# Whitening products of the last stage: six of eight as 64x64 parts, in place of four of eight

## The chip, the cores and the metric

The kernel runs on one core of a Trainium2 chip. The core has a matrix engine (TensorE, PE in the profile), a vector engine (VectorE, DVE), a scalar engine (ScalarE, ACT), GpSimd (POOL) and a queue engine (SyncE, SP) that here only issues DMA transfers. TensorE writes its products into PSUM, a memory of eight banks of 512 float32 for each of 128 partitions; VectorE or ScalarE move them from there into SBUF, which is called an eviction here; DMA carries SBUF to and from HBM.

The metric is the time of one execution on the device in microseconds (us), as the median of several. A profile is one further execution, taken by the hardware profiler, and has its own time.

## The reference

Everything is float32. The input x has 4 images of 256 channels and 64 x 64 pixels. Two layers follow one another. The first is a local attention: a dilated 7 x 7 convolution (256 to 128 channels) and a 1 x 1 convolution (128 to 49) give 49 logits for each pixel, a softmax over the 49 gives weights, and the output is the weighted sum of 49 shifted copies of x. The second layer whitens the result over groups of 64 channels:

```python
x = jnp.transpose(X, (1, 0, 2, 3)).reshape(g, nc, -1)      # g = 4 groups of nc = 64 channels
xc = x - x.mean(-1, keepdims=True)
Sigma = EPS * I + jnp.einsum('gdm,gem->gde', xc, xc) / m
rTr = (1.0 / jnp.einsum('gii->g', Sigma))[:, None, None]
Sigma_N = Sigma * rTr
P = I
for _ in range(T_ITERS):                                    # 5
    P3 = jnp.einsum('gij,gjk,gkl->gil', P, P, P)
    P = 1.5 * P - 0.5 * jnp.einsum('gij,gjk->gik', P3, Sigma_N)
xn = jnp.einsum('gde,gem->gdm', P * jnp.sqrt(rTr), xc)      # the last stage of the kernel
```

then multiplies by a weight and adds a bias for each channel. The covariance is a sum over all pixels of all images, so the last einsum can begin only when the whole attention layer is done.

## The kernel before

**Layout.** Channels lie on the 128 partitions, in two blocks of 128 (`cc`), and each block holds two whitening groups of 64. The attention output stays in SBUF in eight tiles, `slots[2*b + pr]`, for image `b` and row parity `pr`: 128 partitions x 2 blocks x 32 rows x 64 columns. Three of them were moved to HBM while the attention ran and come back as `back` tiles.

**Stages.** The convolutions and the attention take most of the time. Then `whiten` (generators for both blocks in turn) makes the matrices: `wm[cc]`, 128 x 128 and block diagonal with a 64 x 64 block for each group, a scale `sc[cc]` and an offset `beta[cc]` for each channel, and `abx[cc]`, which is scale and offset with the two groups' partitions exchanged. The last stage multiplies every pixel by `wm` and stores the result.

**The last stage (L1410 to L1457).** Its loops run over 4 images, 2 channel blocks and `q` in (0, 2): 16 groups. A group covers 16 rows of each parity, as four products of 128 channels x 512 pixels: `y[pr][k]`, with parity `pr` and half `k`. It gathers them in two SBUF tiles `st[0]` and `st[1]`, 128 x 8 x 2 x 64, of which each is stored by one transfer of 512 KB (`store(k)`, on SP's queue). The `out` pool has six such tiles.

A product is made in one of two ways:
- *plain* (`plain(k)`, L1429): one 128 x 128 matmul into a one-bank tile `tp` (three of them), and one eviction of 128 x 512 with `sc` and `beta`.
- *as parts* (L1445): since `wm` is block diagonal, only its two 64 x 64 blocks matter. Two products are made at once, by four 64 x 64 matmuls, one in each quarter of the array. For `k = 0` group G0 goes to PSUM partitions 0 to 63 and G1 to 64 to 127 (*straight*). For `k = 1` the groups cross: G0's result lands on G1's partitions and the other way round. The straight bank is evicted in one instruction of 128 x 512. The crossed bank needs two instructions of 64 x 512, one for each half, since each writes to other partitions than it reads, with `abx`.

In every group before the change, the two products of parity 0 are plain and the two of parity 1 are parts.

**PSUM.** Parts use two banks, a *set* here. There are two sets: a two-bank tile `apply`, taken anew from a pool with one buffer, and the two long-lived one-bank tiles `cv`. `two_banks` gives them out in turn, so before the change the sets alternate from group to group.

**What sets the order.** `pe(...)` keeps TensorE's instructions in program order. `out_rows` (L1393 to L1398) gives evictions to ScalarE and VectorE in turn, counting all of them: odd to ScalarE, even to VectorE. In which order each of the two engines then takes its evictions is decided by the framework's planner when the kernel is built, from its own costs; each engine runs its queue strictly in that order. The framework also adds all the waits between engines, among them those that keep two engines from reading one PSUM bank at a time, and the wait of a matmul for the evictions that empty its bank.

The matmuls are float32, and each is carried out as two weight loads and two passes of 512 columns: the profile counts a plain product as two MATMUL rows and the four parts as eight.

Of the kernel before, what the change touches and what calls it, by code (L numbers as in the profile page):

```python
# [32 lines left out]
def kernel(  # L33
# [29 lines left out]
    nc = tc.nc  # L63
# [28 lines left out]
    def pe(ins):  # L92
        return tc.keep_in_program_order(ins)
# [9 lines left out]
    def tp():  # L103
        return ps_tp.tile([P, 512], F32, tag="tp", name="tp")
# [19 lines left out]
    store = []  # L124
# [27 lines left out]
    t = tp()  # L152
# [3 lines left out]
    t = tp()  # L156
# [5 lines left out]
    for k in range(2):  # L162
        t = ps_cv.tile([P, 512], F32, name=f"cv{k}")
# [53 lines left out]
    for k, c0 in enumerate(range(0, P, CB)):  # L217
        n = min(CB, P - c0)
        t = cv_buf[k % 2]
        for cc in range(NCC):  # L220
# [5 lines left out]
                    start=True, stop=True,  # L226
# [8 lines left out]
    for k0 in range(0, KT, TB):  # L235
        n = min(TB, KT - k0)
        t = tp()
# [1056 lines left out]
    wm, sc, beta, abx = {}, {}, {}, {}  # L1294
# [98 lines left out]
    def out_rows(o, i, scale, bias):  # L1393
        n[0] += 1
        if n[0] % 2:
            nc.scalar.activation(o, i, AF.Identity, bias=bias, scale=scale)
        else:
            nc.vector.tensor_scalar(o, i, scale, bias, ALU.mult, ALU.add)  # L1398

    def two_banks():  # L1400
        while True:
            t = ps_y.tile([P, 2, NT], F32, tag="y", name="apply")
            yield [t[:, k] for k in range(2)]
            yield cv_buf

    G0, G1 = slice(0, GW), slice(GW, P)
    two = two_banks()
    for b in (3, 2, 1, 0):
        for cc in range(NCC):
            for q in range(0, SH // TR, 2):  # L1410
                st = [
                    rpool.tile([P, TR, 2, W], F32, tag="out", name=f"out_{b}_{cc}_{q + k}", bufs=6)
                    for k in range(2)
                ]
                y = [
                    [
                        slots[2 * b + pr][:, cc, (q + k) * TR : (q + k + 1) * TR, :].rearrange(
                            "p r w -> p (r w)"
                        )
                        for k in range(2)  # L1420
                    ]
                    for pr in range(2)
                ]
                rows_of = lambda t: t.rearrange("p (r w) -> p r w", w=W)
                ts = next(two)

                def plain(k):
                    t = tp()
                    pe(nc.tensor.matmul(t, wm[cc], y[0][k], start=True, stop=True))  # L1429
                    out_rows(st[k][:, :, 0, :], rows_of(t), sc[cc], beta[cc])  # L1430

                def store(k):
                    nc.sync.dma_start(
                        out[
                            b, cc * P : (cc + 1) * P, 2 * (q + k) * TR : 2 * (q + k + 1) * TR, :
                        ],
                        st[k].rearrange("p r two w -> p (r two) w"),
                    )

                plain(0)  # L1440
                for k in range(2):
                    for i in (G0, G1):
                        o = i if k == 0 else (G1 if i is G0 else G0)
                        pe(
                            nc.tensor.matmul(  # L1445
                                ts[k][o], wm[cc][i, i], y[1][k][i],
                                start=True, stop=True, skip_group_check=True,
                            )
                        )
                out_rows(st[0][:, :, 1, :], rows_of(ts[0]), sc[cc], beta[cc])  # L1450
                store(0)
                for i, o in ((G1, G0), (G0, G1)):
                    out_rows(
                        st[1][o][:, :, 1, :], rows_of(ts[1])[i], abx[cc][i, 0:1], abx[cc][i, 1:2]
                    )
                plain(1)
                store(1)  # L1457


# [29 lines left out]
```

## Time and profile before

| what | value |
|---|---|
| median of 3 runs | 747.56 us (745.64 to 749.41) |
| the profiled execution | 746.19 us, of which the span from first to last instruction is 744.4 us |
| busy over the span | PE 94%, PEld 71%, DVE 82%, ACT 45%, POOL 7% |
| first matmul of the last stage | 689.5 us from the span's start |
| first and last store issued | 693.9 and 739.7 us |
| last eviction ends | 739.6 us |
| granted TensorE clock | 0.5 from 690.1 to 693.5 us, then full to 741.3 us |
| stores of the stage | 32 of 512 KB, 16.8 MB |

Times inside the profile are counted from the span's start. PE rows are matmul passes, PEld rows weight loads. A row of the timeline gives start, duration, engine, source line, operation, output<-input, shapes and count, and in brackets how long the engine stood idle before and what ended that. Consecutive alike instructions are merged into one row (x4, x8). The end of a matmul is modelled, so that the distance between the starts of matmuls is the better measure of their cost.

### The profile page before, as it was taken

Reading aid. Unit: us, or ns where it says so; the run is one execution under the profiler, and the core shown is the slowest. Engines: PE = TensorE matmul, PEld = TensorE weight load, DVE = VectorE, ACT = ScalarE, POOL = GpSimd, SP = SyncE. Lnnn points to the kernel's source line nnn. Section 1 sums busy time; section 2 is a strip of 40 time slices with the busy share of each in tenths; the row PEclk is TensorE's granted clock in tenths of the full one; section 3 lists DMA queues with packets and bytes.
Section 4 is the critical chain, followed back from the end, with each engine's and each line's share of the span. In section 5 each row is a group of like instructions: output and inputs, shape, how many; then the busy total and the mean of one; then the engine's idle time right before and its main releaser. Section 6 shows DMA issues by size and latency. Waiting matters only on the chain.

```text
span 744.4 us, 18491 instructions
## 1 busy us (share of the span) xinstructions
PE 703.4 (94%) x7512; PEld 528.3 (71%) x7512; DVE 611.3 (82%) x1268; ACT 332.5 (45%) x953; POOL 51.6 (7%) x52
## 2 busy tenths in 40 slices
PE   6999999997999897999999999999999889998996
PEld 1449543377898794799998958898998678885331
DVE  3789998999999989968995999799969655535575
ACT  1424240255364543466444435735535663322564
POOL 0410070020001110001000100000000000000000
PEclk9999999999899999999999999999999999999999
DMA  8991120147263491076545820534423144371588
GB/s 319 250 319 73 60 88 12 60 147 212 87 193 112 146 317 48 21 245 199 185 128 201 253 69 7 166 108 135 155 64 95 32 149 118 104 296 72 219 357 327
DMA packets 59629, 114.41 MB, mean 154 GB/s; under 512 B 22887, under 2 KB 42008, under 8 KB 58776
## 3 DMA queue, kind: packets, MB, share of 16 engines
q1 hardware_dynamic: 55848, 94.36, 38.7%
q0 software_dynamic: 3696, 18.88, 7.3%
q8 instruction: 59, 0.97, 0.5%
q14 instruction: 26, 0.21, 0.1%
HBM read 65.88 MB, written 47.33 MB: 152 GB/s over the span
## 4 chain that ended last, share of the span: by engine, by line
PE 61%; DVE 28%; ACT 4%; issue 3%; DMA 2%; SPq 0%; DVEq 0%; ACTq 0%
PE cv L538 20%; PE y L1061 12%; PE acc L685 6%; PE tp L1429 4%; PE tp L1093 3%; PE sig L1114 3%; PE cv L685 3%; PE tp L1032 3%; DVE xh L313 3%; DVE pv L313 3%; DVE zz L313 2%; DVE rb L313 2%; PE cv L222 2%; DVE ct L313 2%; DVE band L1009 2%
## 5 line engine op out<-in xcount | busy, mean ns | idle before, releaser
L538 PE MATMUL cv<-xh,wr 128*49 128x128 f32 x4368 | 250.2, 276 | 5.7 <-DVE rm L899 5.3
L538 PEld LDWEIGHTS cv<-xh,wr 128*49 128x49 f32 x4368 | 244.1, 124 | 9.6 <-ACT xh L494 5.5
L1061 PE MATMUL y<-band,xb 128*128 128x224 f32 (+2 forms) x640 | 150.6, 373 | 7.6 <-ACT xb L1040 5.9
L1061 PEld LDWEIGHTS y<-band,xb 128*128 128x128 f32 x640 | 109.1, 192 | 29.0 <-ACT xb L1040 8.9
L548 ACT COPY pv<-cv 113x486 f32<-113x486 f32 (+1 forms) x63 | 30.0, 476 | 86.1 <-PE cv L538 85.8
L1080 ACT ACTIVATE slot<-y,pivot 128x512 f32<-128x512 f32 x53 | 36.6, 738 | 63.5 <-PE y L1061 63.4
L1101 ACT COPY yt<-tp 128x256 f32<-128x256 f32 x128 | 45.6, 378 | 38.8 <-PE tp L1093 37.6
L1032 PE MATMUL tp<-ident,slot 128*128 128x128 f32 x256 | 49.9, 297 | 6.7 <-ACT yt L1101 6.7
L313 DVE SCALAR_TENSOR_TENSOR pv<-pv 113x162 f32<-113x162 f32 x186 | 54.9, 318 | 1.0 <-ACT pv L548 0.4
L1093 PE MATMUL tp<-ident,slot 128*128 128x128 f32 x256 | 52.1, 299 | 3.6 <-ACT yt L1101 1.0
L1009 DVE STREAM_TRANSPOSE band<-band 128x864 f32<-128x864 f32 (+1 forms) x48 | 47.4, 990 | 9.5 <-DMA band<-sd 9.5
L1093 PEld LDWEIGHTS tp<-ident,slot 128*128 128x128 f32 x256 | 41.3, 205 | 13.8 <-issue 4.4
L1032 PEld LDWEIGHTS tp<-ident,slot 128*128 128x128 f32 x256 | 39.9, 205 | 13.0 <-ACT yt L1101 8.0
L941 ACT COPY zt<-d 32x112 f32<-32x112 f32 (+2 forms) x156 | 44.8, 287 | 1.9
L893 ACT ACTIVATE d<-tp,mx 128x49 f32<-128x49 f32 x128 | 37.0, 336 | 17.4 <-DVE mx L888 13.9
L313 DVE SCALAR_TENSOR_TENSOR xh<-ct 128x512 f32<-128x512 f32 x42 | 27.8, 683 | 14.1 <-PE cv L538 13.7
L1114 PE MATMUL sig<-yt 128*64 128x65 f32 x1024 | 36.9, 225 | 0.0
L1114 PEld LDWEIGHTS sig<-yt 128*64 128x64 f32 x1024 | 32.4, 137 | 6.0 <-issue 4.5
L1040 ACT COPY xb<-tp 128x256 f32<-128x256 f32 x87 | 30.5, 376 | 12.9 <-PE tp L1032 12.4
L1040 DVE COPY xb<-tp 128x256 f32<-128x256 f32 x41 | 16.5, 421 | 23.5 <-PE tp L1032 23.5
L685 PE MATMUL acc<-slot,tap 128*49 128x496 f32 (+3 forms) x168 | 34.6, 569 | 0.0
L893 ACT ACTIVATION_READ_ACCUMULATOR d<-tp,mx 128x1 f32 x128 | 30.6, 241 | 0.0
(222 smaller groups left out, 959.2 us busy)
## 6 DMA issues: line engine op xcount, KB each, us to landing
out_dram<-out SPq DMA_DIRECT2D x32, 512.0 KB, 3.4
sd<-zt SPq DMA_DIRECT2D x16, 896.0 KB, 4.2
slot<-in_x_dram POOLq DMA_DIRECT2D x12, 1024.0 KB, 10.0
band<-sd SPq DMA_DIRECT2D x128, 84.0 KB, 2.2
wr<-gd SPq DMA_DIRECT2D x15, 588.0 KB, 3.7
wr<-gd SPq DMA_DIRECT2D x15, 490.0 KB, 3.9
spill<-slot POOLq DMA_DIRECT2D x3, 2048.0 KB, 7.7
back<-spill SPq DMA_DIRECT2D x3, 2048.0 KB, 13.3
```

The costliest lines, as they stand in the source:

```text
L313: return in_turn(STT(o, a, f, b, ALU.mult, ALU.add))
L538: nc.tensor.matmul(cv[h * HB : h * HB + KT, k, sr : sr + n, sc : sc + n], wv[:, sc, sr, cc], xh[bc][:, :n, h * NCC + cc, :n], start=(j == ...
L685: nc.tensor.matmul(ps[h * HB : h * HB + KT, :, w0:w1_], w[v][:, cc], xs[:, :, cc, w0 + d : w1_ + d], start=(j == 0), stop=(j == len(order) ...
L893: nc.scalar.activation(d[:, h, i], lt[i // NI][:, i % NI, h, :KT], AF.Exp, bias=mx[:, i, h : h + 1], accum_out=s[:, h, i : i + 1],)
L941: ins = nc.scalar.copy(o, i)
L1009: return nc.vector.transpose(f, f)
L1032: nc.tensor.transpose(t[:, cc * P : (cc + 1) * P], xt[:, cc, CR * m : CR * (m + 1), bass.ds(pc, SW, 2)], ident,)
L1040: (nc.vector.tensor_copy if tail else nc.scalar.copy)(xb, t[:, :C])
L1061: nc.tensor.matmul(ps[:, cc, q0 - half * HALF : q1 - half * HALF, :], xb[:, cc * P : (cc + 1) * P], rhs, start=(k == 0), stop=(k == len(PI ...
L1093: nc.tensor.transpose(t[:, cc * P : (cc + 1) * P], yt[:, cc, CR * i : CR * (i + 1), bass.ds(pc, SW, 2)], ident,)
L1101: nc.scalar.copy(yb.rearrange("p a g c -> p (a g) c")[:, :, :GW], t[:, :C].rearrange("p (e c) -> p e c", c=GW),)
L1114: nc.tensor.matmul(sig[g * GW : (g + 1) * GW, cc], yb[:, cc, g, :GW], yb[:, cc, g], start=(count[0] == 0 and cc == 0), stop=(count[0] == 4 ...
```

## The change

Groups come in pairs, `q = 0` and `q = 2`. In groups with `q = 2` nothing changes. In groups with `q = 0` the two parity-0 products become parts as well: first the four parts of parity 0 into one set, then the four parts of parity 1 into the other set. Then come two straight evictions, the store of `st[0]`, four crossed evictions of half a bank, and the store of `st[1]`. Six of eight products of a pair are parts then, in place of four.

A group of `q = 0` takes two sets and one of `q = 2` takes one, three for a pair. With A and B for the sets, TensorE's order over two pairs is:

- before: plain, A, plain | plain, B, plain | plain, A, plain | plain, B, plain
- after: A, B | plain, A, plain | B, A | plain, B, plain

A pair has 11 evictions in place of 10, so ScalarE and VectorE change roles from pair to pair.

```diff
-                ts = next(two)
 
                 def plain(k):
                     t = tp()
                     pe(nc.tensor.matmul(t, wm[cc], y[0][k], start=True, stop=True))
                     out_rows(st[k][:, :, 0, :], rows_of(t), sc[cc], beta[cc])
+
+                def parts(pr):
+                    t = next(two)
+                    for k in range(2):
+                        for i in (G0, G1):
+                            o = i if k == 0 else (G1 if i is G0 else G0)
+                            pe(
+                                nc.tensor.matmul(
+                                    t[k][o], wm[cc][i, i], y[pr][k][i],
+                                    start=True, stop=True, skip_group_check=True,
+                                )
+                            )
+                    return t
+
+                def straight(t, pr):
+                    out_rows(st[0][:, :, pr, :], rows_of(t[0]), sc[cc], beta[cc])
+
+                def crossed(t, pr):
+                    for i, o in ((G1, G0), (G0, G1)):
+                        out_rows(
+                            st[1][o][:, :, pr, :], rows_of(t[1])[i],
+                            abx[cc][i, 0:1], abx[cc][i, 1:2],
+                        )
...
+                if q:
+                    plain(0)
+                    t = parts(1)
+                    straight(t, 1)
+                    store(0)
+                    crossed(t, 1)
+                    plain(1)
+                    store(1)
+                else:
+                    t = [parts(pr) for pr in range(2)]
+                    for pr in range(2):
+                        straight(t[pr], pr)
+                    store(0)
+                    for pr in range(2):
+                        crossed(t[pr], pr)
+                    store(1)
```

The lines that the last block replaces did for every group what the branch `if q:` does now.

More of the change, by code (lines that the diff above doesn't have):

```diff
@@ L1438, in store @@
                     )
[L1440 to L1457, printed above, removed]
+                if q:
[14 more added lines that the diff above has]
+                    store(1)
 _INS = [
```

## The prediction

> **What bounds the kernel now.** The page first, busy times and the chain that ended last:
>
> ```profile
> PE 703.4 (94%) x7512; PEld 528.3 (71%) x7512; DVE 611.3 (82%) x1268; ACT 332.5 (45%) x953; POOL 51.6 (7%) x52
> ...
> PE 61%; DVE 28%; ACT 4%; issue 3%; DMA 2%; SPq 0%; DVEq 0%; ACTq 0%
> ```
>
> TensorE leads both, but these are averages over all stages. The change touches only the stage from 689.5 us to the end at 744.4. The stage table, for four pairs of groups in the steady part of it:
>
> ```profile
> core 0: us, PE busy (x) PEld busy (x) DVE busy (x) ACT busy (x) POOL busy (x), PEclk, DMA share, GB/s
> 703.96:727.42 23.46, 23.46 (x100) 7.08 (x103) 16.17 (x21) 15.50 (x21) 0.00 (x0) 1.00 0.88 358
> ```
>
> TensorE never stands still: a pair takes 23.46 / 4 = 5.87 us. VectorE and ScalarE are busy for two thirds. DMA is not far behind (share 0.88). Then one pair in the timeline:
>
> ```profile
> 727.35 1.09 PE L1445 MATMUL apply<-back,PS 64*64 64x512 f32 x8
> 728.37 1.98 PE L1429 MATMUL tp<-back,PS 128*128 128x512 f32 x4
> 728.51 0.81 DVE L1398 TENSOR_SCALAR out<-apply,ab 128x512 f32<-128x512 f32 x1 [0.65 <-PE apply L1445]
> ...
> 729.59 0.78 ACT L1396 ACTIVATE out<-tp,ab 128x512 f32<-128x512 f32 x1 [0.90 <-ACT out L1396]
> 730.28 1.09 PE L1445 MATMUL cv<-back,PS 64*64 64x512 f32 x8
> 730.39 0.77 ACT L1396 ACTIVATE out<-apply,abx 64x512 f32<-64x512 f32 x1
> 730.39 0.81 DVE L1398 TENSOR_SCALAR out<-tp,ab 128x512 f32<-128x512 f32 x1 [1.07 <-PE tp L1429]
> 731.24 0.80 DVE L1398 TENSOR_SCALAR out<-apply,abx 64x512 f32<-64x512 f32 x1
> 731.30 1.98 PE L1429 MATMUL tp<-back,PS 128*128 128x512 f32 x4
> 731.46 0.78 ACT L1396 ACTIVATE out<-cv,ab 128x512 f32<-128x512 f32 x1 [0.30 <-ACT out L1396]
> 732.07 0.82 DVE L1398 TENSOR_SCALAR out<-cv,abx 64x512 f32<-64x512 f32 x1
> ...
> 732.97 0.77 ACT L1396 ACTIVATE out<-cv,abx 64x512 f32<-64x512 f32 x1 [0.74 <-DVE out L1398]
> 733.22 1.09 PE L1445 MATMUL apply<-back,PS 64*64 64x512 f32 x8
> ```
>
> Two things are to be seen. Starts give the costs: parts take 728.37 - 727.35 = 1.02 us for two products, two plain products 1.91. Second, how long a set stays occupied. The apply set is written by 728.37. Its straight bank is read at 728.51, its halves only at 730.39 and, after the first half, at 731.24; it is empty at 732.04, 3.67 us after its parts. The cv set (parts over at 731.30) is empty at 733.74, 2.44 us after. Nobody waits for that now: apply is written again at 733.22, 4.85 us after its last parts.
>
> The wait list for the same stretch confirms that the second half waits for the first, on the other engine:
>
> ```profile
> ACT out L1396 <- DVE out L1398: 4.0, 5, 1.0
> ```
>
> In apply the roles are exchanged, VectorE starting 0.08 us after ScalarE's half ends (731.16, 731.24). ScalarE's apply half also carries a wait on VectorE's semaphore in the trace, which I read as the straight eviction; in cv there is none, and there the first half (732.07) overlaps the straight one (731.46 to 732.24).
>
> [...] a product as a part costs 0.51 us against 0.96, its evictions no less (0.77 to 0.82 for a half bank, 0.78 to 0.81 for a whole). [...]
>
> **The change, part by part.**
>
> *TensorE's own work.* A pass costs 0.43 us (plain passes start that far apart). Before, a pair has four plain products of two passes and two sets of parts of two passes, 12 passes = 5.16 us; the other 0.71 is four mode changes, 0.18 each. After: four passes of parts, two plain, two parts, two plain: 10 passes, still four mode changes, 5.01 us. Gain 0.86 a pair, times 8 pairs = **6.9 us** for TensorE alone. The half-clock window covers the first four passes in both.
>
> *Evictions.* 11 for a pair instead of 10; eight more of about 0.8 over two engines, 4.5 us of each in a pair. That still fits under 5.01, so their number alone costs nothing; without TensorE's cover they would bound the pair at 4.5.
>
> *Stores.* Still 32. The DMA view's best slices move 418 GB/s, so a pair's 2.1 MB need 5.0 us: TensorE's new 5.01 just covers it. From the first store (693.9, about the same: four passes and two evictions lie before it in either version) DMA could end at about 693.9 + 1.4 (2.6 shortest landing less 1.25 transfer) + 40.1 = 735.4, so it does not forbid the gain.
>
> *The sets: a new wait.* A set was used once in two groups; now three uses in two groups, and A is wanted again soon, twice.
>
> First reuse, in every pair: A's parts, then B's parts (two passes) and one plain product (two passes) with two mode changes, some 4 x 0.43 + 0.3 = 2.0 us after A's first parts. A's shortest emptying: 0.25 until its data is seen (0.59 modelled pass plus 0.09 to the engine, less 0.43), straight 0.78 and first half 0.78, both on the same engine by the turn count, 0.08 to the other engine, second half 0.81, 0.09 back to TensorE: 2.8 us. Stall 0.8, eight times: 6.4.
>
> Second reuse: the set that the `q = 2` group used is the second one of the next pair. TensorE has a plain product and two passes of parts between, 2.1 us. If the set is apply, where straight, first half and second half follow each other on alternating engines: 0.25 + 0.81 + 0.08 + 0.77 + 0.08 + 0.81 + 0.09 = 2.9, stall 0.8, at four of the seven passages: 3.3. If it is cv, straight and first half overlap and it is 2.0: nothing.
>
> So with queues that never put anything else first, the stage changes by -6.9 + 6.4 + 3.3 = **+2.8 us**.
>
> *Queue order.* The planner's order now is not of that kind. ScalarE stands idle until 729.59 for the plain eviction and takes the apply half after it, although the straight one ended at 729.32; VectorE too takes a plain eviction before its half. Against the shortest 2.8 (parts over to empty, without the 0.11 of the mode change) the apply set takes 3.67, one eviction more; cv takes 2.44, half of one more. After the change there are twelve reuses where this counts. Bounds: none of them delayed, 0; all delayed by one eviction of 0.82, 9.8. I take four, 3.3, since a stall also gives the engines time to catch up and since the other set's evictions, which stand between, must be done anyway.
>
> *Behind the waiting matmul* are plain(1), its eviction, `store(1)` and the next pair's parts, all late by the same stall. The three `tp` tiles now serve two products a pair, and six `out` tiles last three groups against landings of 3.4 us: neither binds.
>
> Sum: -6.9 + 6.4 + 3.3 + 3.3 = **+6.1 us**. The profiled execution becomes a span of 750.5 and a time of 752.3; on the median shown, 1.4 above that execution, 753.7. I give 753.0.
>
> **Rivals.** 0.5% is 3.7 us, about what a measurement of this kernel tells from no change.
> 1. *Only the unavoidable chain.* Evictions are taken as they come: +2.8, some 750; or the stalls are a little shorter and cancel the gain, 747. For it: the planner will see the tight reuse in its own schedule. Against: its present order.
> 2. *The gain arrives.* If the halves of a bank are read side by side, the chain of 2.8 falls by 0.9 to 1.9, below the 2.0 of cover; the stalls go and 6.9 us are gained: 740.5. It decides at 2.0. [...] Against: the 0.08 between halves, and the waits that the program carries on both sets.
> 3. *Every reuse is delayed by a foreign eviction*: +12.6, 760. One more window at half clock would have the same effect in part: eight passes at 0.43 more than now, if at all 1.7 us a window. Against: TensorE would still be busy for three quarters.
>
> **How the numbers follow.** Forecast, +4 to +10 (751 to 757): 0.55. Rival 1: 0.22, rival 2: 0.09, rival 3: 0.14. Slower by over 0.5% is the forecast and rival 3, 0.69; within 0.5% is rival 1, 0.22; faster 0.09. The range leaves out rival 2, a few per cent at the low end of rival 1 and the far end of rival 3: 746.5 to 759.
>
> **What would show it.** Right: the stage table falls below full PE time, with a pair at some 6.6 us instead of 5.87; the parts' weight loads waiting 0.8 us or more for the last eviction of the same set, at the eight first reuses and at apply's second ones; the plain products' rows halved from 64 to 32, and a lower DMA share. Wrong: no such waits and a pair near 5.0 us (rival 2); waits in every pair near 1.6 us (rival 3); a second 0.5 clock window; or parts following parts that cost more than 0.43 us a pass, which nothing in the profile of before shows.

## The result

The changed kernel takes 756.08 us (median of 4, 754.42 to 756.53) against 747.2 us (median of 4, 745.64 to 749.41). The medians lie 8.9 us apart; the ratio estimated from the runs is 1.0109 with a 95% interval of 1.0091 to 1.0126, so the change costs between 6.8 and 9.4 us. The time lies in the stated range, 3.1 us above the forecast of 753.0.

Where the time went is read by pairs of groups. The stage table of the changed kernel, one line for each of five pairs that follow one another (columns as in the prediction):

```profile
707.61:713.52 5.91, 5.08 (x29) 1.40 (x28) 3.95 (x5) 3.77 (x5) 0.00 (x0) 1.00 0.81 333
713.52:722.24 8.72, 6.89 (x29) 1.45 (x29) 4.88 (x6) 4.48 (x6) 0.00 (x0) 0.80 0.59 239
722.24:728.15 5.91, 5.23 (x30) 1.49 (x29) 3.95 (x5) 3.94 (x6) 0.00 (x0) 1.00 0.89 361
728.15:735.20 7.05, 5.22 (x29) 1.25 (x28) 4.10 (x6) 3.95 (x6) 0.00 (x0) 1.00 0.58 239
735.21:741.50 6.29, 5.88 (x29) 1.51 (x28) 4.72 (x6) 4.46 (x6) 0.00 (x0) 1.00 0.95 387
```

Two kinds alternate. Pairs that begin with apply (first channel block) take 5.91 us, 0.9 more than their own 5.01 of TensorE work; the one at 735.21 takes 6.29, 1.3 more, and the experiment with the filler shows why. Pairs that begin with cv take 7.05, which is 2.04 more. Two of the latter, at 698.91 and 713.52, ran with a mean clock of 0.80 and took 8.70 and 8.72. In two 5.91 pairs and the 7.05 pair TensorE is busy for 5.08 to 5.23 us: its work did shrink, and it waits.

In this profile the granted clock is 0.5 for 3.41 us at a time while the stage's matmuls run (a half-clock window here): from 692.75 to 696.17, in the first pair, and from 702.99 to 706.41 and 716.65 to 720.06, in the two of 8.70 and 8.72.

The sum over the eight pairs: the four that begin with cv wait 2.04 us each, 8.2 in all, and the four that begin with apply wait 0.2 (the first), 0.9, 0.9 and 1.3, which is 3.3. Two pairs with a half-clock window took 1.66 longer each, another 3.3. With TensorE's own gain that is 8.2 + 3.3 + 3.3 - 6.9 = 7.9, and the stage itself, from its first matmul to the end of the span, grew by 7.9 (62.8 against 54.9). The remaining 2.5 us between the two profiled executions lie before the stage, where the whitening ran at half clock for 6.8 us in this execution (679.1 to 685.9) and for 3.4 in the other (679.9 to 683.3). The code there is the same. In the seven profiles of this document that share it the stage begins anywhere from 689.2 to 692.6 us, so these 2.5 us are not put down to the change.

The list of waits of the changed kernel over the stage shows VectorE waiting for parts and parts waiting for VectorE:

```profile
DVE out L1398 <- PE cv L1437: 10.0, 8, 2.8
PE apply L1437 <- DVE out L1398: 9.4, 8, 1.8
```

Parts written to apply wait for VectorE in all eight pairs: 1.83 us in each of the four that begin with cv, and 0.17 to 0.83 in the others. Why the wait is so long where cv comes first, the timeline of the pair at 728.15 shows:

```profile
727.22 0.81 DVE L1398 TENSOR_SCALAR out<-apply,ab 128x512 f32<-128x512 f32 x1 [0.58 <-PE apply L1437]
728.15 0.21 PEld L1437 LDWEIGHTS cv<-back,PS 64*64 64x64 f32 x8 [0.76 <-issue]
728.15 1.09 PE L1437 MATMUL cv<-back,PS 64*64 64x512 f32 x8
728.30 0.78 ACT L1396 ACTIVATE out<-tp,ab 128x512 f32<-128x512 f32 x1 [1.81 <-issue]
729.11 0.78 ACT L1396 ACTIVATE out<-apply,abx 64x512 f32<-64x512 f32 x1
729.27 0.81 DVE L1398 TENSOR_SCALAR out<-cv,ab 128x512 f32<-128x512 f32 x1 [1.24 <-PE cv L1437]
730.12 0.80 DVE L1398 TENSOR_SCALAR out<-apply,abx 64x512 f32<-64x512 f32 x1
...
731.06 1.09 PE L1437 MATMUL apply<-slot,PS 64*64 64x512 f32 x8 [1.83 <-DVE out L1398]
```

The apply set was written just before 727.09. Its straight bank is evicted from 727.22 to 728.03, and ScalarE could then take the first half. It takes the plain product (728.30) first and the half at 729.11. VectorE waits 1.24 us for cv, evicts cv's straight bank, and only then takes apply's second half. That ends at 730.92, and the parts start at 731.06, 2.91 us after the parts before them where 0.91 would do. So both foreign evictions stand in front, one on each engine. ScalarE's is the dear one: with the 0.08 us from one engine to the other that the prediction read, the first half could have begun at 728.11, 1.0 us earlier. VectorE's costs 0.15, since the second half could not begin before the first was done (729.97 in place of 730.12). With the 0.8 that the shortest chain costs in any case, that makes the 2.0.

### The profile page after: what moved, and what is told of

It reads as the page before. It is cut to its first block, busy times and chain, and to the rows that moved or that the text cites. A ratio compares the mean times of both kernels' runs of the same rounds, so it can differ in the third digit from the quotient of the medians.

```text
span 754.8 us, 18575 instructions
## 1 busy us (share of the span) xinstructions
PE 704.1 (93%) x7544; PEld 527.1 (70%) x7544; DVE 614.4 (81%) x1272; ACT 334.9 (44%) x957; POOL 51.3 (7%) x52
## 4 chain that ended last, share of the span: by engine, by line
PE 59%; DVE 27%; ACT 5%; DMA 4%; issue 3%; SPq 1%; DVEq 0%; ACTq 0%
PE cv L538 19%; PE y L1061 12%; PE acc L685 6%; PE tp L1093 3%; PE sig L1114 3%; PE cv L685 3%; PE tp L1032 3%; DVE pv L313 2%; DMA band<-sd 2%; DVE xh L313 2%; DVE zz L313 2%; DVE rb L313 2%; PE cv L222 2%; DVE band L1009 2%; DVE out L1398 2%
```

## The experiments

Each ratio is against runs of the kernel before that were timed together with the experiment; their median was 747.82 us for the first four experiments and 748.52 for the others.

**A third set.** The parts of `q = 2` groups go to two `tp` banks; apply and cv are each used once in a pair.

```diff
                 def parts(pr):
-                    t = next(two)
+                    t = [tp(), tp()] if q else next(two)
```

> Edit: the changed kernel, but the parts of a q = 2 group go to two tp banks, so that each of the sets apply and cv is used once in a pair. Theory (TensorE waits for a set to be emptied): with no set wanted again before 4 us, the waits of about 0.9 us in even pairs and 2.0 us in odd pairs go, a pair comes to 5.0 to 5.2 us for TensorE or for the stores, the half-clock windows inside the stage go too, and the time falls by 12 to 15 us against the changed kernel, to 741 to 744, below the kernel before (747). Rival (parts that follow parts are dearer than 0.43 us a pass, or 11 evictions bound the pair): the pairs stay near 5.9 and 7.1 us and the time at 754 to 757.

Measured: 743.37 us (median of 8), ratio to the kernel before 0.9935 (0.9912 to 0.9959). Two pairs of its stage table:

```profile
703.88:709.24 5.36, 5.08 (x29) 1.32 (x28) 4.02 (x6) 4.37 (x6) 0.00 (x0) 1.00 0.93 379
709.24:714.75 5.51, 5.08 (x29) 1.32 (x28) 4.72 (x6) 3.96 (x6) 0.00 (x0) 1.00 0.96 390
```

The same matmuls and the same number of evictions, and the loss has become a gain. Parts behind parts are not dear (0.91 us apart), and eleven evictions do not bound a pair at 5.9. What cost the time was the early reuse of a set, though the planner also made new queues here; the runs in written order below hold the order fixed. The pairs are not at 5.0 to 5.2 as expected but at 5.36 and 5.51, because the second plain product waits for a `tp` bank; the run with an eighth bank takes that up.

**The queues in written order.** As the changed kernel, but each engine takes its evictions in the order in which they are written (`pe` is the wrapper that keeps program order).

```diff
-            nc.scalar.activation(o, i, AF.Identity, bias=bias, scale=scale)
+            pe(nc.scalar.activation(o, i, AF.Identity, bias=bias, scale=scale))
         else:
-            nc.vector.tensor_scalar(o, i, scale, bias, ALU.mult, ALU.add)
+            pe(nc.vector.tensor_scalar(o, i, scale, bias, ALU.mult, ALU.add))
```

> Edit: the changed kernel, but ScalarE and VectorE take the evictions in the order in which they are written; the sets as in the changed kernel. Theory with the queue order as its second part: in odd pairs VectorE no longer puts the next pair's straight eviction of cv ahead of apply's second half, the wait of 2.0 us there falls to 0.8 or 0.9, the one in even pairs stays at 0.8 or 0.9; 4 x 1.1 = 4.4 us less than the changed kernel, about 751.5, and 3.3 less again (748) if the shorter waits keep the clock up. Rival (the shortest chain alone makes the waits, the order does not matter): 755 to 757.

Measured: 748.88 us (median of 12), ratio 1.0016 (0.9996 to 1.0037). Its stage table and the timeline of the second of these pairs:

```profile
704.36:710.27 5.91, 5.08 (x29) 1.44 (x29) 3.95 (x5) 3.77 (x6) 0.00 (x0) 1.00 0.91 374
710.27:716.80 6.53, 5.99 (x29) 1.40 (x29) 4.88 (x6) 4.64 (x7) 0.00 (x0) 1.00 0.75 301
```

```profile
710.24 0.77 ACT L1396 ACTIVATE out<-apply,abx 64x512 f32<-64x512 f32 x1 [1.63 <-issue]
710.27 0.21 PEld L1437 LDWEIGHTS cv<-slot,PS 64*64 64x64 f32 x8 [0.76 <-issue]
710.27 1.09 PE L1437 MATMUL cv<-slot,PS 64*64 64x512 f32 x8
711.04 0.78 ACT L1396 ACTIVATE out<-tp,ab 128x512 f32<-128x512 f32 x1
711.05 0.80 DVE L1398 TENSOR_SCALAR out<-apply,abx 64x512 f32<-64x512 f32 x1 [0.89 <-ACT out L1396]
711.88 0.81 DVE L1398 TENSOR_SCALAR out<-cv,ab 128x512 f32<-128x512 f32 x1
711.90 0.21 PEld L1437 LDWEIGHTS apply<-slot,PS 64*64 64x64 f32 x8 [1.43 <-DVE out L1398]
...
713.98 1.83 PE L1437 MATMUL cv<-slot,PS 64*64 64x512 f32 x8
...
715.75 1.12 PE L1428 MATMUL tp<-slot,PS 128*128 128x512 f32 x2
```

ScalarE now takes apply's first half (710.24) before the plain product, and VectorE the second half before cv's straight bank. In this pair the parts into apply start 1.63 us after those before them instead of 2.91, so the wait there fell from 2.0 to 0.7. In its place the first reuse of cv shows: from its parts to the next product 1.77 us go by instead of 1.02, another 0.75. In the other pairs the first reuse of apply costs 0.9. Over all eight pairs, by the starts of the matmuls, the first reuses cost 6.5 us, the second ones of apply 2.9 and those of cv nothing. The prediction worked out 6.4, 3.3 and nothing for queues that put nothing else first. There is no half-clock window inside this stage after its first: the granted clock is 1.00 in the pairs above, and 0.985 over the execution against 0.977 in the changed kernel. From the start of its first matmul to the start of its last, the stage grew by 2.6 us over the kernel before. From there to the end it is 1.1 shorter (5.6 us instead of 6.7), so less of this is seen in the time.

**One-bank tiles.** As the changed kernel, with apply as two tiles of one bank each, taken from a new pool after the old one is given back.

```diff
-            t = ps_y.tile([P, 2, NT], F32, tag="y", name="apply")
-            yield [t[:, k] for k in range(2)]
+            yield [
+                ps_two.tile([P, NT], F32, tag=f"ap{k}", name=f"apply{k}") for k in range(2)
+            ]
```

> Edit: the changed kernel, but apply becomes two tiles of one bank each, as cv is, so that apply's first half need not wait for its straight eviction. Theory: the second reuse of apply in odd pairs is then like cv's, with a chain of about 2.0 us under 2.1 us of cover, so 4 x 2.0 = 8 us less, 748, less the clock windows 3.3 us, 745; the first reuse in every pair stays exposed and may now appear in odd pairs as well with 0.8 us each (+3), so 745 to 750. Rival (that wait is of no consequence): 754 to 757.

Measured: 746.3 us (median of 20), ratio 0.9971 (0.9957 to 0.9985). The stage table:

```profile
707.47:713.38 5.91, 5.91 (x29) 1.67 (x28) 5.20 (x7) 3.58 (x5) 0.00 (x0) 1.00 0.89 358
713.38:719.09 5.71, 5.71 (x30) 1.67 (x29) 3.63 (x5) 4.83 (x7) 0.00 (x0) 1.00 0.90 368
```

TensorE shows no idle time here because the two products of a set are emptied and refilled one at a time, so that one runs while the other waits (parts into apply start at 708.38, while VectorE reads its other bank from 707.91 to 708.71); each pair is still 0.7 to 0.9 us above 5.01. The wait of apply's first half for the straight eviction, which the prediction had only read off a semaphore, shows in the overlaps: in the changed kernel the straight eviction of apply overlaps a half in none of twelve uses, and here it does in four. How much of the gain comes from that is not shown. TensorE can now refill one bank while the other is still being emptied, and the planner arranged the queues otherwise, so this run changes three things.

**A filler for the clock.** As the changed kernel, with two more 64 x 64 matmuls between the two sets of parts when `cc = 1`, into a `tp` bank that is never read.

```diff
-                    t = [parts(pr) for pr in range(2)]
+                    t = [parts(0)]
+                    idle = tp() if cc else None
+                    for i in (G0, G1) if cc else ():
+                        pe(nc.tensor.matmul(idle[i], wm[cc][i, i], y[0][0][i],
+                                            start=True, stop=True, skip_group_check=True))
+                    t.append(parts(1))
```

> Edit: the changed kernel with work added: in odd pairs (cc = 1), between the two sets of parts, two more 64x64 matmuls of 512 columns into a tp bank that nobody reads, 0.86 us of TensorE work inside a wait of 2.0 us. Theory of the clock (the waits let the clock fall to half in two windows of 3.4 us, at 1.66 us each): the waits stay, the windows go, 3 us less than the changed kernel, 753. Rival (the clock does not matter, or the filler only adds work): 756 or up to 3.4 us more, 759.

Measured: 754.3 us (median of 6), ratio 1.008 (1.005 to 1.0109), against 1.0109 for the changed kernel. The intervals overlap, so the times alone do not settle it. The granted clock says more: its mean over an execution is 0.981 to 0.987 in the six runs with the filler and 0.977 to 0.981 in the four of the changed kernel. The stage table of the profiled execution:

```profile
711.56:718.63 7.07, 6.08 (x33) 1.53 (x32) 4.11 (x6) 3.97 (x6) 0.00 (x0) 1.00 0.62 248
718.63:724.92 6.29, 5.88 (x30) 1.52 (x29) 4.72 (x6) 4.45 (x6) 0.00 (x0) 1.00 0.96 389
```

The long pair is as long as without the filler (7.05): 0.86 us of added TensorE work is free inside the wait. The clock stays full through the stage after its first 3.4 us (1.00 in both pairs above and in the next, to 731.98). The short pairs take 6.2 to 6.3 us in place of 5.91. The changed kernel's own pair at 735.21 shows the same and why:

```profile
735.95 0.31 PEld L1437 LDWEIGHTS cv<-back,PS 64*64 64x64 f32 x4 [0.53 <-ACT out L1396]
...
736.12 1.84 PE L1437 MATMUL cv<-back,PS 64*64 64x512 f32 x8
...
736.89 0.20 PEld L1437 LDWEIGHTS cv<-back,PS 64*64 64x64 f32 x4 [0.63 <-ACT out L1396]
...
737.90 1.12 PE L1428 MATMUL tp<-back,PS 128*128 128x512 f32 x2
```

The second reuse of cv, which the prediction put at nothing, waits for ScalarE: 1.78 us go by from these parts to the next product, where parts that do not wait take 0.97 (708.52 to 709.49). In the changed kernel this is the one pair of its kind that follows a pair at full clock. Behind a pair with a half-clock window the wait is 0.2 us or less; that the slower TensorE gives the evictions time to catch up is an estimate, from the 1.90 us between a plain product and the next parts inside a window (702.84 to 704.74), where 1.06 go by at full clock (732.08 to 733.14). By it a half-clock window also saves some 0.35 us in the next pair, and the sum for the filler is -3.3 for two windows, +0.7 for two such pairs and +0.6 in the first pair of the stage: -2.0 us, which is what the stage gained (60.7 against 62.8).

In the changed kernel itself, the six changes of the granted clock from 692.75 to 720.06 us lie whole multiples of 3.41 us apart. Its stage table in stretches on the same grid:

```profile
699.58:702.99 3.41, 1.58 (x13) 0.39 (x10) 2.43 (x3) 1.41 (x3) 0.00 (x0) 1.00 0.51 210
713.23:716.65 3.42, 1.59 (x13) 0.45 (x16) 2.11 (x4) 1.55 (x2) 0.00 (x0) 1.00 0.63 260
726.89:730.30 3.41, 2.35 (x14) 0.51 (x10) 1.80 (x3) 1.55 (x2) 0.00 (x0) 1.00 0.86 347
740.54:743.95 3.41, 2.05 (x10) 0.41 (x10) 2.10 (x3) 1.55 (x2) 0.00 (x0) 1.00 0.89 365
702.99:706.41 3.42, 3.42 (x10) 0.55 (x10) 1.63 (x2) 1.90 (x3) 0.00 (x0) 0.50 0.61 250
```

The first two stretches, with TensorE busy for 1.58 and 1.59 us of 3.41, are followed by the two half-clock windows; the last line is the first of these. The third and fourth, busy for 2.35 and 2.05 us, are not. A wait of 2.0 us falls into each of the four, but only in the first two does the whole of it lie inside one stretch.

The busy share alone does not decide, though. In the kernel before, the 3.41 us ahead of the stage's half-clock window (690.12 to 693.53) hold mostly thin matmuls of the whitening, of 1 to 256 columns, and TensorE was busy for 83% of it:

```profile
686.71:690.12 3.41, 2.83 (x15) 1.93 (x14) 1.93 (x10) 0.12 (x1) 0.00 (x0) 1.00 0.00 0
```

What the clock goes by is thus not shown here. The link from the long waits to the two windows rests on the stretches above and on the filler, with which the longest wait of the parts is 1.0 us, so that a stretch of 3.41 us with a long wait is 71% busy or more.

**The halves apart.** As the changed kernel, but each crossed half has a bank of its own, the third of a set from `tp`. Both sets are used as early as in the changed kernel.

```diff
-                    t = next(two)
+                    t = [*next(two), tp()]
...
-                                    t[k][o], wm[cc][i, i], y[pr][k][i],
+                                    t[2 if k and i is G1 else k][o], wm[cc][i, i], y[pr][k][i],
...
-                            st[1][o][:, :, pr, :], rows_of(t[1])[i],
+                            st[1][o][:, :, pr, :], rows_of(t[1 if i is G1 else 2])[i],
```

> Edit: the changed kernel, but each crossed half of a set goes to a bank of its own (the third from the tp banks), so that both engines may evict the two halves at once; the sets apply and cv are used as in the changed kernel. Theory (the two halves, one after the other on two engines, make the chain longer than the cover): the chain falls by 0.9 us to 1.9 or 2.0, below the cover of 2.0 to 2.1, so most of the waits of 0.9 and 2.0 us go; a pair at 5.0 to 5.6 us, the time at 741 to 746. Rival (the queue order holds the banks whether or not the halves wait for each other): 750 to 756. The tp banks now serve five products of a pair, which may leave a few tenths of waiting in each.

Measured: 741.87 us (median of 4), ratio 0.9926 (0.9901 to 0.9952). From its timeline and its stage table:

```profile
704.96 0.81 DVE L1398 TENSOR_SCALAR out<-apply,ab 128x512 f32<-128x512 f32 x1
705.80 0.80 DVE L1398 TENSOR_SCALAR out<-tp,abx 64x512 f32<-64x512 f32 x1
705.86 0.77 ACT L1396 ACTIVATE out<-apply,abx 64x512 f32<-64x512 f32 x1 [0.73 <-ACT out L1396]
```

```profile
703.82:708.92 5.10, 5.07 (x29) 1.31 (x28) 4.27 (x6) 4.26 (x6) 0.00 (x0) 1.00 1.01 406
708.92:713.93 5.01, 5.01 (x29) 1.52 (x28) 4.36 (x6) 4.16 (x7) 0.00 (x0) 1.00 0.96 388
```

The two halves now run side by side (705.80 and 705.86), and the pairs fall to 5.10 and 5.01 (one of those not shown takes 5.39). With the sets reused as early as before, shortening the chain by one half's eviction is enough. That half's bank comes from the `tp` banks, so the next parts into apply or cv need not wait for it at all. Since the planner makes new queues for every kernel, it cannot be said how much of this is the shorter chain and how much a better order that it allows.

**An eighth bank.** The third set, and the second plain product goes into the bank of the covariance sums, which is free by then. Its tile is made a whole bank for that; that line and the one of the third set are left out here.

```diff
-                    t = tp()
+                    t = sig_bank if k else tp()
```

> Edit: the third set of the first series, and the second plain product of a group goes into the bank of the covariance sums, which is free by then, instead of a tp bank. In the first series a pair took 5.44 us, and TensorE still waited 0.35 to 0.51 us before that product for the tp bank of the first one. Theory: that wait goes, a pair comes to 5.0 to 5.1 us, 8 x 0.4 = 3 us less than the 743.4 of the third set, 740. Rival (stores of 5.0 us a pair or the evictions already hold the pair near 5.4): 743.

Measured: 742.58 us (median of 4), ratio 0.9931 (0.9912 to 0.995).

```profile
703.76:708.77 5.01, 5.01 (x29) 1.32 (x29) 3.95 (x6) 4.65 (x7) 0.00 (x0) 1.00 0.98 401
708.77:713.78 5.01, 5.01 (x30) 1.32 (x29) 4.79 (x7) 3.68 (x6) 0.00 (x0) 1.00 1.00 403
```

TensorE does not wait in these pairs, and a pair takes the 5.01 us that the prediction counted, with the DMA share at 0.98 and 1.00. Against the third set alone (0.9935) the ratio is not resolved: the pairs are 0.4 us shorter, but the intervals overlap almost wholly, and the 3 us expected of it are not seen in the time. The profiles show where they went. From the start of the stage's first matmul to the start of its last 41.2 us go by, 3.0 fewer than with the third set alone, but from there to the end 7.8 instead of 5.7. With the DMA share at 0.98 to 1.00, a store lands 4.5 us after its issue (median), with the third set alone 3.2 and in the changed kernel 2.6. The stores now end well behind TensorE, so the expectation's rival was right for the time and wrong for the pairs.

**The same in written order**, to see whether order matters without early reuse:

> Edit: as the eighth-bank kernel, and the evictions in the order in which they are written. Theory (with no set wanted again soon the queue order no longer matters): within 1 us of the eighth-bank kernel, 740. Rival (order is a cost of its own): 3 us or more apart.

Measured: 741.79 us (median of 4), ratio 0.9916 (0.989 to 0.9941), pairs of 5.01: no difference from the eighth bank that can be told. Set beside the changed kernel in written order (1.0016, pairs of 5.91 and 6.53), this run also settles what the planner's freedom left open in the others. Both keep the order in which the evictions are written, and only the banks differ. With more banks the waits are gone.

**The kernel before in written order:**

> Edit: the kernel before, with the evictions in the order in which they are written. Theory (the queue order counts only where a set is wanted again within its chain; before the change there are 4.85 us against 3.67): no difference to the kernel before, within 0.3%. Rival (order is a cost of its own): 2 us or more less.

Measured: 746.73 us (median of 12), ratio 0.998 (0.9969 to 0.9991). That is inside the 0.3%, though the interval excludes no difference. A pair takes 5.86 us, as in the kernel before (5.87), so the 0.2% is not in the steady part; where it is was not found.

## Why the prediction was right, and where it was off

*TensorE's own work, -6.9 us*: right. With the waits gone a pair takes 5.01 us, ten passes of 0.43 and four mode changes (0.18 each by the prediction's estimate), and parts behind parts, 0.91 us apart, add nothing to that.

*Eviction count and stores as no bound*: right for the pairs. Three versions with 11 evictions a pair reach 5.0 to 5.1 us, but for a single pair of 5.39, with a DMA share of 0.96 to 1.01 in the pairs shown. In the time the stores do take back a part, as the eighth bank shows.

*The waits for a set, +6.4 and +3.3*: right in kind and in size, as the run in written order shows (6.5 and 2.9). That kernel is the first rival, forecast at +2.8 against a kernel like the one before. Its matmuls take 2.6 us longer, and its time measured 1.0016, some 1.2 us, with an interval up to 2.8; set against the kernel before in the same written order (0.998) it is 2.7.

*Queue order, +3.3*: right in kind, and the foreign eviction is there by name. The distribution was not as predicted: all four reuses of apply in pairs that begin with cv were hit, by 2.0 us in place of 0.8, and the first reuses of cv vanished behind them. The second reuses of cv, put at nothing, cost up to 0.8. In sum the changed kernel's waits are 11.5 us against the forecast's 13.0, or +4.6 net against +6.1, and 2.1 more than in written order. The sum fits better than its parts, since a delay at one reuse spares the next a wait; that the two came out so close is partly luck.

*The clock*: left out of the sum, and the step that failed. It stood only in the third rival, with a price (1.7 us a window, measured 1.66; that is four passes at 0.43 more, where the text says eight) and, against it, that TensorE would still be busy for three quarters: an estimate that nothing in the profile of before ties to the clock. It holds for a pair (5.22 of 7.05 us) but not for the 3.41 us ahead of each of the two half-clock windows, which the long wait of 2.0 us, in one piece, left 46% busy. Two windows, 3.3 us in the profiled execution, are what takes the stage's +4.6 to +7.9. They are also one of the signs by which the prediction wanted to be found wrong. The other executions have no timeline, but their mean clock is lower as well: 0.977 to 0.981, against 0.982 to 0.987 in 37 runs of the kernel before. So the 3.1 us above the forecast are not one error: waits of 1.5 us less and a clock loss of 3.3 that was not counted make 1.8, and the rest lies outside the stage or in the scatter between executions.

*Rival 2, the halves side by side*: seen where the program puts them in different banks (705.80 and 705.86 with the halves apart). In the changed kernel they were chained, as the prediction read from the kernel before: ScalarE's half ran from 729.11 to 729.89, VectorE's from 730.12, and in neither profile do two halves of one bank overlap. Whether they could is not shown.

## What to carry to other kernels

Before making an engine faster, take from the timeline how long each PSUM set stays occupied from its last matmul to its last eviction, and compare it with the TensorE work that will lie between two uses after the change; here the chain of 2.8 us met a cover of 2.0. The set stayed occupied longer, so the gain turned into a wait, and more banks, or one bank for each evicting engine, brought it back: with a third set or separate halves the same matmuls ended 0.7% below the kernel before. Look in the queue of each evicting engine for what stands in front of the last eviction of a set.

## What the runs showed of the hardware

In the changed kernel two waits on TensorE cost more than their length: two windows of 3.41 us that TensorE spent 46% busy were each followed by one at half clock, while windows at 60% and 69% were not, and the pair around each half-clock window took 1.66 us longer. 0.86 us of unread matmuls put into each wait of this kind left no half-clock window after the stage's first in the profiled execution (1.00 from 711.56 to 731.98; 0.985 over the execution against 0.977). No threshold follows: in the kernel before, 3.41 us of mostly thin matmuls, 83% busy, were followed by half clock too.

Evictions of 64 and 128 partitions took the same time (0.76 to 0.82 us). Two engines reading different banks of one set overlapped almost fully (0.74 us of 0.77, with the halves apart).
